# A two-layer cross-attention and feed-forward kernel: weight rows broadcast in two halves, second weights beside Gelu, last two tails transposed on TensorE, expert weights loaded a group earlier

## The chip, the cores and the metric

The kernel runs on one core of one Trainium2 chip, as one launch. The metric is device time in microseconds; the time of a kernel is the median of several executions. All arithmetic is in float32.

## The reference, cut to what matters

There are 16 sequences of 256 rows of width 256, `x`, and as many of context, `ctx`. Four stages follow one another, each added to the residual:

```
x = x + cross_attention_0(ctx, layernorm(x))   # 8 heads of 128; keys and values from ctx and x together (512 rows)
x = x + ffn_0(layernorm(x))                    # 256 -> 1024 -> 256, Gelu; see below
x = x + cross_attention_1(layernorm(x), ctx)   # one head of 256
x = x + experts(layernorm(x))                  # 8 gated experts of width 256, a weighted sum of those a row chooses
```

The first feed-forward has weights of its own for every sequence: to the shared `W1` and `W2` a small product of that sequence's own rows is added,

```
lt = y[:, 1:17, :];  even = lt[:, ::2];  odd = lt[:, 1::2]
m1 = (even[:, :4, :, None] * odd[:, :4, None, :]).reshape(B, 1024, 256)
m2 = (even[:, 4:, :, None] * odd[:, 4:, None, :]).reshape(B, 256, 1024)
h   = gelu(y @ W1.T + scale * y @ m1.T + b1)
out = h @ W2.T + scale * h @ m2.T + b2
```

so that sixteen rows of the normalised `y` have to be known everywhere before the feed-forward of that sequence can begin.

## The kernel before, in words

The order of the work on every engine is written out by the program; nothing is reordered at run time. The main loop goes over 128 heads, `n = 8 b + h`, sequence ("batch") after batch. For a head, `s0q` and `s0k` make queries and keys (TensorE tiles `pq`, `pk`), `s1` the scores (`sc`) and their maxima (`nm`, VectorE) and exponentials (`pr`, ScalarE), `s1_scale` divides the rows by their sums on GpSimd (L864), and `s2` transposes the result in blocks of 32 on VectorE into `tb` and sends it to DRAM (`hop`, L876); `s2_fetch` brings it back fully transposed (`pT`, four DMAs, L885), and `s3` multiplies it with the values (`po`, into `outT`). `tb` has one buffer: the next head's block transposes wait until the store of the one before has landed. `values` makes the values of half the heads at a time (`pv`), a tile at a time, as filler.

Between these steps the loop leaves gaps (`gap`), in which jobs run for the batches before: `chain(b)`, which carries batch b from the output projection (`px`) through both feed-forward matmuls (`ph`, `pf`), the second attention (`pv1`, `pq1`, `sc1`, `po1`) and the last layer norm, and `route(b)`, which picks experts and scatters rows with indirect DMAs from GpSimd (`slots_d`, L683). A job yields a number: the TensorE time, by the program's own count `Clock.pe`, after which its next step may be placed. `Clock.pe` is a planner's guess made when the program is built; on the chip each engine runs its own list in order and waits for semaphores. All plain DMAs are issued from one queue, SyncE's ("SP"), in order.

The chain of a batch transposes its four row blocks in the same way as the heads, by `to_blocks` (VectorE, then a store to DRAM) and `from_blocks` (four fetches): `yb` to `ybT`, `yc` to `ycT`, `pr1` to `pr1T`, `row` to `ydT`. The planner allows `SENT` = 6.5 us before the fetch and `LANDED` = 7.5 us after it.

For the first feed-forward the chain writes the sixteen rows of `y` to DRAM (`ev_d`) and reads them back into all 128 partitions, 8 KB each, by one DMA `ev<-ev_d` of 1 MB (L384). That DMA is issued right behind a head's four `pT` fetches, by the list `behind_fetch`. VectorE then builds the batch's first weights `W1e` (L412, two instructions for every two of the eight `ph` tiles) and GpSimd and VectorE its second ones, `W2e` (L419, L427), interleaved with the `ph` matmuls. Gelu (L459) is one ScalarE instruction over all of `hT`, and needs another activation table than the exponentials.

When the heads are done, the experts' part (`experts`) takes over TensorE: groups of up to four tiles of 128 rows, expert after expert, in two parts (the first ten batches, the last six). A group's rows are read from `slots_d` (L1091), transposed by the same hop over DRAM, and put through gate, up and down matmuls (`pg`, `pu`, `pd`); VectorE scales the result into a tile `o` (L1173), and GpSimd adds it to the output by an indirect DMA (L1174). An expert's weights `wx` are loaded two groups ahead of their use (L1074 to L1076). The rows of the second part may be loaded only when the last batch's `route` has scattered all of its slots. The chains of the last two batches run beside the first experts.

Of the kernel before, what the change touches and what calls it, by code (L numbers as in the profile page):

```python
# [12 lines left out]
F32 = mybir.dt.float32  # L13
# [6 lines left out]
P = 128  # L20
# [9 lines left out]
def xattn_ffn_kernel(  # L30
# [301 lines left out]
    def chain(b, A, behind):  # L332
# [8 lines left out]
        def mv_tile(tag):  # L341
            return small.tile([P, TC, 2], F32, tag=f"mv{tag}", bufs=2, name=f"mv_{tag}_{b}")

        def raw_tile(tag, name):
            return wk.tile([P, QP, DC, TC, QB], F32, tag=tag, name=name)

        mv = mv_tile("b")
# [25 lines left out]
        nc.vector.tensor_copy(yp, y[0:32, 0, :].rearrange("p (a c) -> p c a", c=NI))  # L373
        hop = to_blocks(wk, y, TC, "tbc", 1, f"yb_{b}_b")
        ev_d = dram.tile([2 * NI, D], F32, tag="ev_d", name=f"ev_d_{b}")
# [6 lines left out]

        def rows_everywhere():
            nc.sync.dma_start(  # L384
                ev.rearrange("p n d -> p (n d)"),
                ev_d.rearrange("n d -> (n d)").partition_broadcast(P),
            )
            landed.append(Clock.pe + 12.0)

        behind_fetch.append(rows_everywhere)  # L390
        plus_row(x_b, lasting["b2"])
        yield SENT
        yTb = raw_tile("yT", f"ybT_{b}")
        from_blocks(yTb, hop)
        yT = in_order(yTb)
        while not landed:
            yield 0.2
        yield max(landed[0] - Clock.pe, LANDED)
        while behind is not None and b - 1 not in A.fed_forward:
# [4 lines left out]
        nc.vector.tensor_scalar(  # L404
            od, yTb[:, 0, :, 0, 2 : 2 + 4 * NI : 2], lasting["scale"], None, ALU.mult
        )
# [25 lines left out]
        w1_rows(0)  # L432
        w2_block(0)
        w1_rows(1)
        yield 4.0 if b < B - 1 else 6.0
        hT = wk.tile([P, HC, S], F32, tag="hT", name=f"hT_{b}")
        for k in range(HC):
            ph = mm_tile(S, f"ph_{b}_{k}")
            for d in range(DC):
                mm(  # L440
                    ph, W1e[:, d].rearrange("p i a -> p (i a)")[:, ts(k, P)], yT[:, d],
                    start=(d == 0), stop=(d == DC - 1),
                )
            nc.vector.tensor_scalar(hT[:, k, :], ph, col("b1", k), None, ALU.add)
            if k % 2 == 1:
                i = k // 2
                if i + 2 < NI:
                    w1_rows(i + 2)
                if i + 1 < NI:
                    w2_block(i + 1)  # L450
                yield 1.0
                w2_add(i)
        A.fed.add(b)
# [8 lines left out]

        behind_exp.append(gelu)
        while not done:
            yield 0.2
# [24 lines left out]
        plus_row(x_b, lasting["bv1"])  # L490
        hop = to_blocks(wk, y, TC, "tbc", 1, f"yc_{b}_b")
        pr = wk.tile([P, TC, S], F32, tag="pr1", name=f"pr1_{b}")
# [5 lines left out]
        for m in range(TC):  # L498
# [4 lines left out]
            yield  # L503
        yield sent - Clock.pe
        yTc = raw_tile("raw_c", f"ycT_{b}")
        from_blocks(yTc, hop)
        landed = Clock.pe + LANDED + 1.5
        for c in range(TC):
# [3 lines left out]
            )  # L512
        yield landed - Clock.pe
        q1T = wk.tile([P, DC, S], F32, tag="q1T", name=f"q1T_{b}")
        for m in range(DC):
            pq = mm_tile(S, f"pq1_{b}_{m}")
            for d in range(DC):
                mm(
                    pq, M1[:, d, ts(m, P)], in_order(yTc)[:, d], start=(d == 0),
                    stop=(d == DC - 1),  # L520
                )
            evict(q1T[:, m, :], pq, u1[:, m : m + 1], QS1)
# [14 lines left out]
        yield 3.0  # L537
        hop = to_blocks(wk, pr, TC, "tbc", 1, f"pr1_{b}_b")
        yield SENT
        raw = raw_tile("raw_c", f"pr1T_{b}")  # L540
        from_blocks(raw, hop)
        yield LANDED
        pT = wk.tile([P, TC, S], F32, tag="pT1", bufs=1, name=f"pT1_{b}")
        for m in range(TC):
            evict(pT[:, m, :], in_order(raw)[:, m], None, None)
        yield 4.0
        mv = mv_tile("d")
# [14 lines left out]

        yield 2.8 if b < B - 1 else 10.0
        while b >= 2 and not A.tails[b - 2].done:
# [3 lines left out]
        nc.vector.tensor_copy(row[:, :, D + E], number[:, b * TC : (b + 1) * TC])  # L568
        hop = to_blocks(wk, row, TC, "tbc", 1, f"yd_{b}_b")
        yield SENT  # L570
        raw = raw_tile("raw_c", f"ydT_{b}")
        from_blocks(raw, hop)
        yield LANDED
        ydT = wk.tile([P, DC, S], F32, tag="q1T", name=f"ydT_{b}")
        for d in range(DC):
            evict(ydT[:, d, :], in_order(raw)[:, d], None, None)
        yield 4.0
        while b >= 1 and b - 1 not in A.weighed:
# [14 lines left out]
    def route(b, A, mine):  # L593
# [87 lines left out]
        for c in range(TC):  # L681
            for e in range(E):
                ins = nc.gpsimd.indirect_dma_start(  # L683
                    out=slots_d[part],
                    out_offset=bass.IndirectOffsetOnAxis(ap=at_slot[:, c, e : e + 1], axis=0),
                    in_=row[:, c, :], in_offset=None,
                )
                apart(ins, f"slots_{part}")
                if e % 2 == 1:
                    yield 2.6  # L690

# [11 lines left out]
    with ExitStack() as sh, ExitStack() as sa, ExitStack() as sf:  # L703
# [315 lines left out]
        def bulk(b, h):  # L1019
            if h == 0:  # L1020
                if b == 0:
                    filling["turns"] = all_turns()
                filling["in"] = inputs(b + 1) if b + 1 < B else None
            if h == 2:
                filling["v1"] = values(b, 1)
            if h == 6:
                filling["v0"] = values(b + 1, 0) if b + 1 < B else None
            if b == 0:
                load_late(h)
                for _ in range(2):  # L1030
                    advance(filling["turns"])
            if 2 <= h <= 5:
                advance(filling["v1"])
            if 1 <= h <= 5:
                advance(filling["in"])
            if h == 7 and b + 2 < B:
                load_in(b + 2)
            if h >= 6:
                advance(filling["v0"])
                yield  # L1040
                advance(filling["v0"])
            yield
# [35 lines left out]
        class G:  # L1078
# [83 lines left out]
            def down(self, t):  # L1162
# [4 lines left out]
                for i in range(IC):  # L1167
# [3 lines left out]
                    )  # L1171
                o = D_.wk.tile([P, D], F32, tag="o", bufs=8, name=f"o_{self.name}_{t}")
                nc.vector.tensor_scalar(o, pd, self.wt[:, t : t + 1], None, ALU.mult)  # L1173
# [9 lines left out]
        def experts(groups, ready=None):  # L1183
# [12 lines left out]
            for n, g in enumerate(groups):  # L1196
# [5 lines left out]
                for i in range(IC):  # L1202
                    g.gate(i)
                    yield
                    g.up(i)
                    yield
                    if n == 0:
                        groups[1].turn_rows(i)
                    if n + 2 < len(groups):
                        if i == 0:  # L1210
                            groups[n + 2].send_rows()
                        else:
                            groups[n + 2].fetch_rows()
                    if i == 0 and n + 3 < len(groups):
                        groups[n + 3].load()
                    if late is not None:
                        late.down(2 * i)
                        late.down(2 * i + 1)
                        yield
                if n + 2 < len(groups) and groups[n + 2].e not in D_.w:  # L1220
                    while len(D_.w) > 1 and D_.more is None:
                        yield 0.4
                    load_expert(groups[n + 2].e)
# [24 lines left out]
        for n in range(NS + 2):  # L1248
# [17 lines left out]
            while behind_exp:  # L1266
                behind_exp.pop()()
            stand = 2.0 if n >= NS - 1 else 0.0
            gap(stand=stand)
            if n < NS:  # L1270
                s1_scale(n)
            if 1 <= n <= NS:
                s2_fetch(n - 1)
            while behind_fetch:
                behind_fetch.pop()()
            if n + 1 < NS:
                s0q(n + 1)
            gap(stand=stand)
            if n + 1 < NS:
                s0k(n + 1)  # L1280
            gap(stand=stand)
            advance(more)
            gap(stand=stand)
            advance(more)
            gap(stand=stand)
            if n >= 2:
                s3(n - 2)
            gap(stand=stand)
            if n < NS:
# [4 lines left out]
        while line:  # L1294
            for late in (behind_exp, behind_fetch):
                while late:
                    late.pop()()
            if D_.more is None and B - 1 in A.projected:
# [52 lines left out]
```

## Time and profile before

| what | value |
|---|---|
| median of 3 runs | 1911.05 us (1908.29 to 1915.36) |
| the profiled execution | 1918.48 us, its span 1916.5 us |
| mean granted TensorE clock over the span | 0.978 |
| TensorE busy | 1837.2 us, 96% of the span |
| VectorE, ScalarE, GpSimd busy | 1215.9, 582.8, 864.8 us |
| bytes moved by DMA | 336.91 MB, mean 176 GB/s |

The profile tells for every instruction when it ran and how long its engine had been idle before, and what ended that idle time. A line of the timeline holds the start in us, the length in us, the engine, the source line, the operation, output and inputs by the program's names, and how many like it were merged; behind that, in brackets, the idle time before it and its releaser. SPq is SyncE's queue, which issues the DMAs. A helper records every matmul, so all have line L80 (transposes L84).

### The profile page before, as it was taken

The page shows a single profiled execution, that of the slowest core. Times are in us where ns is not written, and L with a number is a line of the kernel's source. Part 1 is how long each engine was busy: PE and PEld are TensorE (multiplying, and loading weights), DVE is VectorE, ACT ScalarE, POOL GpSimd, SP SyncE. Part 2 cuts the span into 40 slices and gives each one's busy share as a digit, 9 for nine tenths or more (in the row PEclk, how much of TensorE's full clock was granted, in tenths as well). Part 3 has the DMA queues.
Part 4 walks back from the last instruction along what each step waited for, and adds up shares of the span by engine and source line. Part 5 has one row for each costly group of instructions (what it writes and reads, how often), then busy time and mean ns, then how long its engine had stood idle before and what let it go on. Part 6 is the DMA issues. An engine that isn't in the chain of part 4 may idle for free. (4 is left out here: it accounts for less than half of the span.)

```text
span 1916.5 us, 22738 instructions
## 1 busy us (share of the span) xinstructions
PE 1837.2 (96%) x6568; PEld 1242.2 (65%) x6568; DVE 1215.9 (63%) x3350; ACT 582.8 (30%) x1297; POOL 864.8 (45%) x996
## 2 busy tenths in 40 slices
PE   8999999999999999899999999999998999998997
PEld 5666666666666666666666666666665766665665
DVE  5465676757676767576767676666665766664554
ACT  3333333333333333333333333333332211110110
POOL 2132325262626262526262626262615285776665
PEclk9999999999999999999999999999998999998998
DMA  6554446363646463636364636363636487998996
GB/s 223 177 176 139 157 132 201 132 202 127 213 132 205 136 208 132 198 126 211 127 211 138 206 132 203 133 206 134 210 107 208 136 226 197 250 255 201 209 208 109
DMA packets 274638, 336.91 MB, mean 176 GB/s; under 512 B 31773, under 2 KB 227273, under 8 KB 272457
## 3 DMA queue, kind: packets, MB, share of 16 engines
q1 hardware_dynamic: 243736, 283.82, 46.7%
q0 software_dynamic: 30720, 51.54, 11.5%
q8 instruction: 55, 0.90, 0.2%
q14 instruction: 79, 0.64, 0.1%
q10 hardware_dynamic: 48, 0.01, 0.0%
HBM read 167.87 MB, written 167.38 MB: 175 GB/s over the span
## 5 line engine op out<-in xcount | busy, mean ns | idle before, releaser
L864 POOL TENSOR_SCALAR pr<-pr,ri 128x512 f32<-128x512 f32 x256 | 178.0, 706 | 436.1 <-DVE ri L863 432.8
L856 ACT ACTIVATE pr<-sc,nm 128x512 f32<-128x512 f32 x256 | 173.7, 683 | 499.1 <-DVE nm L850 473.9
L683 POOL DMA_INDIRECT slots_d<-row,at_slot x256 | 254.7, 995 | 68.9 <-issue 67.9
L80 PE MATMUL po<-pT,v 128*128 128x256 f32 x1024 | 249.9, 388 | 4.0 <-DMA pT<-hop 4.0
L80 PEld LDWEIGHTS po<-pT,v 128*128 128x128 f32 x1024 | 201.3, 197 | 68.5 <-issue 33.2
L1174 POOL DMA_INDIRECT out_dram<-o,at x128 | 200.6, 1567 | 97.0 <-DVE o L1173 39.9
L80 PE MATMUL sc<-kT,qT 128*128 128x512 f32 x512 | 240.9, 593 | 0.0
L80 PE MATMUL pk<-kvT,Wk_sb 128*128 128x512 f32 x512 | 240.6, 592 | 0.0
L80 PE MATMUL pv<-Wv_sb,kvT 128*128 128x512 f32 x512 | 237.4, 592 | 0.0
L872 DVE STREAM_TRANSPOSE tb<-pr 128x512 f32<-128x512 f32 x256 | 165.7, 685 | 69.2 <-DMA hop<-tb 49.4
L80 PE MATMUL ph<-ybT,W1e 128*128 128x256 f32 x512 | 140.0, 418 | 38.0 <-DVE W1e L412 35.4
L850 DVE TENSOR_REDUCE nm<-sc 128x1 f32<-128x512 f32 x256 | 161.9, 666 | 15.8 <-PE sc L80 15.8
L80 PEld LDWEIGHTS pv<-Wv_sb,kvT 128*128 128x128 f32 x512 | 97.0, 190 | 102.2 <-issue 96.6
L80 PEld LDWEIGHTS ph<-ybT,W1e 128*128 128x128 f32 x512 | 103.7, 207 | 88.0 <-issue 65.5
L902 DVE TENSOR_SCALAR outT<-po,cvec 128x256 f32<-128x256 f32 x128 | 60.7, 474 | 149.2 <-PE po L80 118.3
L80 PE MATMUL pg<-yTd,wx 128*128 128x384 f32 (+3 forms) x328 | 127.8, 513 | 16.0 <-DVE o L1173 11.8
L80 PEld LDWEIGHTS pk<-kvT,Wk_sb 128*128 128x128 f32 x512 | 97.4, 190 | 68.0 <-issue 61.2
L80 PEld LDWEIGHTS sc<-kT,qT 128*128 128x128 f32 x512 | 97.0, 190 | 68.1 <-issue 61.2
L80 PE MATMUL pq<-kvT,Wq_sb 128*128 128x256 f32 x512 | 133.5, 383 | 0.0
L1149 ACT ACTIVATE sg<-pg 128x384 f32<-128x384 f32 (+3 forms) x82 | 41.3, 504 | 294.1 <-PE pg L80 239.6
L80 PE MATMUL pu<-yTd,wx 128*128 128x384 f32 (+3 forms) x328 | 126.2, 508 | 0.0
L80 PE MATMUL pd<-wx,hTd 128*128 128x256 f32 x512 | 124.3, 380 | 2.0 <-DVE hTd L1160 2.0
(191 smaller groups left out, 2659.1 us busy)
## 6 DMA issues: line engine op xcount, KB each, us to landing
hop<-tb SPq DMA_DIRECT2D x128, 512.0 KB
pT<-hop SPq DMA_DIRECT2D x512, 128.0 KB
ev<-ev_d SPq DMA_DIRECT2D x16, 1024.0 KB
rows<-slots_d SPq DMA_DIRECT2D x31, 397.5 KB
hop_rows_b<-rows_b SPq DMA_DIRECT2D x30, 384.0 KB
yTd<-hop_rows_b SPq DMA_DIRECT2D x120, 96.0 KB
rows<-slots_d SPq DMA_DIRECT2D x8, 530.0 KB
cin<-in_ctx_dram SPq DMA_DIRECT2D x16, 256.0 KB
```

The lines of the kernel that those rows point to most:

```text
L80: nc.tensor.matmul(out, lhsT, rhs, **kw)
L683: ins = nc.gpsimd.indirect_dma_start(out=slots_d[part], out_offset=bass.IndirectOffsetOnAxis(ap=at_slot[:, c, e : e + 1], axis=0), in_=row ...
L850: nc.vector.tensor_reduce(nm, sc, AX.X, ALU.max, negate=True)
L856: nc.scalar.activation(pr, sc, AF.Exp, bias=nm, accum_out=sm)
L864: nc.gpsimd.tensor_scalar(pr, pr, ri, 1.0, ALU.mult, ALU.mult)
L872: nc.vector.transpose(tb[:, :, c, :], heads[n][c][0].rearrange("p (m f) -> p m f", m=QP))
L902: nc.vector.tensor_scalar(o, po, col("bv", h), None, ALU.add)
L1149: nc.scalar.activation(self.sg, self.pg, AF.Tanh, scale=0.5)
L1174: ins = nc.gpsimd.indirect_dma_start(out=out_rows[0 : sum(NTOKS[: self.part + 1]), :], out_offset=bass.IndirectOffsetOnAxis(ap=self.at[:, ...
```

## The change

The broadcast `ev<-ev_d` becomes two DMAs of 512 KB, the rows for the first weights and those for the second, and `behind_fetch` gives out only one a head, so the second stands behind the next head's `pT` fetches. The building of `W2e` moves from between the `ph` tiles to behind the placing of Gelu. The `ph` tiles are planned 6.0 instead of 4.0 us behind the first `W1e` instructions. One tile of `values` moves from head 2 of each batch to head 5, which now places two. For the last two batches (`hopped` is false) the four hops over DRAM are replaced by `turned_tile`: four TensorE transposes into PSUM and one ScalarE copy each. `route` of the last two batches places its sixteen scatters at twice the distance. The experts' weights are loaded up to three groups ahead. `o` gets a ninth buffer, and the gaps in the last three steps of the loop take in at least 2.6 us of other work.

```diff
+        hopped = b < B - 2
+        def turned_tile(src, tag, name):
+            t = wk.tile([P, DC, S], F32, tag=tag, bufs=1, name=name)
+            nc.scalar.copy(t, transposed(src, f"{name}_p"))
+            return t
...
-        hop = to_blocks(wk, y, TC, "tbc", 1, f"yb_{b}_b")
+        if hopped:
+            hop = to_blocks(wk, y, TC, "tbc", 1, f"yb_{b}_b")
...
-        def rows_everywhere():
+        def rows_everywhere(half):
             nc.sync.dma_start(
-                ev.rearrange("p n d -> p (n d)"),
-                ev_d.rearrange("n d -> (n d)").partition_broadcast(P),
+                ev[:, ts(half, NI)].rearrange("p n d -> p (n d)"),
+                ev_d[ts(half, NI)].rearrange("n d -> (n d)").partition_broadcast(P),
             )
-            landed.append(Clock.pe + 12.0)
-        behind_fetch.append(rows_everywhere)
+            landed.append(Clock.pe + 8.0)
+        behind_fetch.extend([lambda: rows_everywhere(0), lambda: rows_everywhere(1)])
...
+            yield 2.2
+            yT = latents = turned_tile(y, "yT", f"ybT_{b}")
...
         w1_rows(0)
-        w2_block(0)
         w1_rows(1)
-        yield 4.0 if b < B - 1 else 6.0
+        yield 6.0
...
                     w1_rows(i + 2)
-                if i + 1 < NI:
-                    w2_block(i + 1)
                 yield 1.0
-                w2_add(i)
...
         behind_exp.append(gelu)
+        while len(landed) < 2:
+            yield 0.2
+        yield landed[1] - Clock.pe
+        for c in range(NI):
+            w2_block(c)
+            yield 1.7
+            w2_add(c)
...
+            yTc = turned_tile(y, "raw_c", f"ycT_{b}")
...
+            pT = turned_tile(pr, "pT1", f"pT1_{b}")
...
-        yield 2.8 if b < B - 1 else 10.0
+        yield 2.8 if b < B - 1 else 6.0
...
+            yield 1.4
+            ydT = turned_tile(row, "q1T", f"ydT_{b}")
...
                 if e % 2 == 1:
-                    yield 2.6
+                    yield 2.6 if b < B - 2 else 5.2
...
-            if h == 2:
+            if h == 3:
                 filling["v1"] = values(b, 1)
...
-            if h >= 6:
-                advance(filling["v0"])
+            if h >= 5:
+                late = filling["v1"] if h == 5 else filling["v0"]
+                if h >= 6:
+                    advance(late)
                 yield
-                advance(filling["v0"])
+                advance(late)
...
-                o = D_.wk.tile([P, D], F32, tag="o", bufs=8, name=f"o_{self.name}_{t}")
+                o = D_.wk.tile([P, D], F32, tag="o", bufs=9, name=f"o_{self.name}_{t}")
...
+                ahead = groups[min(n + 3, len(groups) - 1)].e
+                if ahead not in D_.w and (len(D_.w) < 2 or D_.more is not None):
+                    load_expert(ahead)
...
-            while behind_fetch:
-                behind_fetch.pop()()
+            if behind_fetch:
+                behind_fetch.pop(0)()
...
-            stand = 2.0 if n >= NS - 1 else 0.0
-            gap(stand=stand)
+            stand, least = (2.0, 2.6) if n >= NS - 1 else (0.0, 0.8)
+            gap(least, stand)
```

## The prediction, made before the changed kernel ran

> **What bounds the kernel now.** I read the page's busy shares first, then the waits of TensorE, then the timeline around the largest of them, then the tail. TensorE is busy 1837.2 of 1916.5 us, so only its idle time, and what follows from it, can be won. The list of its waits, by line and releaser:
>
> ```profile
> PE ph L80 <- DVE W1e L412: 35.4, 13, 5.0
> PE pg L80 <- DVE o L1173: 11.8, 2, 8.6
> ...
> PE pg L80 <- DMA wx<-in_L_ffn_Wg_dram: 4.1, 2, 2.7
> PE po L80 <- DMA pT<-hop: 4.0, 1, 4.0
> ```
>
> One wait recurs in nearly every batch: the first `ph` waits for its weights `W1e`. The timelines of three engines show why, in batch 5 (start, length):
>
> ```profile
> 593.66 0.36 SPq L384 DMA_DIRECT2D ev<-ev_d  x1
> 597.70 0.67 SPq L876 DMA_DIRECT2D hop<-tb  x1
> 604.98 1.76 SPq L885 DMA_DIRECT2D pT<-hop  x4
> 606.78 1.92 SPq L302 DMA_DIRECT2D pr1T<-hop_pr_b  x4
> 605.02 1.30 DVE L872 STREAM_TRANSPOSE tb<-pr 128x512 f32<-128x512 f32 x2 [4.56 <-DMA hop<-tb]
> 607.67 2.38 DVE L412 SCALAR_TENSOR_TENSOR W1e<-ev,od,W1T 128x256 f32<-128x256 f32 x4
> 604.07 1.88 PE L80 MATMUL pv<-Wv_sb,kvT 128*128 128x512 f32 x4
> 608.26 3.63 PE L80 MATMUL ph<-ybT,W1e 128*128 128x256 f32 x8 [2.31 <-DVE W1e L412]
> 613.60 1.89 PE L80 MATMUL po<-v,pT 128*128 128x256 f32 x8
> ```
>
> `ev` is issued at 593.66, the store `hop<-tb` behind it at 597.70. VectorE cannot write `tb` before that store has landed and waits 4.56 us for it, to 605.02. The maxima, `od` and `W1e` stand behind on VectorE, so `ph` starts 2.31 us late. Then comes a second loss: eight `ph` matmuls take 3.63 us where eight `po` take 1.89. The windows show the granted clock and the DMA share (columns: window, length, busy us and count of PE, PEld, DVE, ACT, POOL, then PEclk, DMA share, GB/s):
>
> ```profile
> 595.00:599.00 4.00, 4.00 (x13) 2.18 (x12) 1.70 (x5) 2.96 (x7) 3.08 (x4) 1.00 0.95 246
> 599.00:605.00 6.00, 6.00 (x20) 3.40 (x19) 0.48 (x1) 1.09 (x2) 4.89 (x7) 1.00 1.05 385
> 608.00:612.00 4.00, 3.74 (x9) 2.80 (x10) 2.75 (x8) 2.13 (x7) 2.98 (x5) 0.58 0.74 212
> 1463.00:1480.00 17.00, 10.88 (x29) 6.97 (x28) 7.73 (x18) 3.58 (x9) 8.15 (x10) 0.70 0.89 248
> 1747.00:1764.00 17.00, 8.43 (x22) 5.04 (x21) 5.63 (x15) 0.49 (x1) 14.13 (x10) 0.70 0.88 188
> ```
>
> The queues are full from 595 to 605, and from 608 to 612 the clock is 0.58. In the trace's clock records 11 of 13 batches (1 to 13) have such a spell at half speed behind the stall, nine of 3.41 and two of 6.83 us: 44.4 us, 22.2 lost. With 35.0 us idle in these batches the loop loses 57 us, 4.4 a batch.
>
> In the tail the same wait and the granted clock recur at 1463 (last batches), and the experts wait for rows:
>
> ```profile
> 1757.17 2.90 PE L80 MATMUL pg<-yTd,wx 128*128 128x384 f32 x4 [8.57 <-DVE o L1173]
> 1755.27 1.10 DVE L291 STREAM_TRANSPOSE rows_b<-rows 128x256 f32<-128x256 f32 x3 [11.97 <-DMA rows<-slots_d]
> ```
>
> The named releaser of the first line is VectorE, but VectorE itself sat 11.97 us until `rows` came, which may be read only after the last `slots_d` scatter: the DMA is the cause.
>
> **The halves and the moved tile.** Window 595 to 599 is the broadcast: some 4.3 us of a full queue. A half takes 2.1 us if time goes with bytes. Two things bring the `tb` store's landing forward: half the broadcast ahead of it (2.1), and the `pv` tile (1.72 us of pitch) that now stands in head 5, not head 2, so that heads 3 to 5 come that much earlier against the chain. Together 3.8 us, more than the 2.31 of the stall: `W1e` is then in time. What is next? On TensorE the order around here is now `pv`, `pv`, `po` of head 3, the second attention's `po1`, `sc`, and only then `ph`, while before `ph` came ahead of `po`. On SyncE half B stands behind the `pT` fetches of the next head and ahead of the four `pr1T` fetches. `po` would be due at 605.95, its `pT` landing at about 606.7: a wait of 0.75. `po1`, due at about 608.4, needs `pT1`, which ScalarE copies from `pr1T`:
>
> ```profile
> 611.53 0.71 ACT L787 COPY pT<-pr1T 128x256 f32<-128x256 f32 x2 [1.87 <-DMA pr1T<-hop_pr_b]
> ```
>
> That copy comes 3.8 us earlier by what is ahead, 2.1 later by half B: at 609.8, ending at 610.5, so `po1` waits about 2 us. The stall moves from `ph` to `po1`.
>
> I put the price on the whole loop by one point, the scores `sc` that follow this stretch. Over the 13 batches, the copy starts on average 18.3 us behind the issue of `ev`, and `sc` 22.5 us. In the changed order `sc` follows the copy by its first tile (0.4) and the two `po1` (1.73): 18.3 − 3.8 + 2.1 = 16.6 for the copy against the old issue, but that issue itself lies 1.7 later against the moved heads, so against the same point of the projection the copy is again at 18.3, and `sc` at 20.4. A wait that brings half speed like those in 11 of 13 batches adds 22.2/13 = 1.7, less the part that was already inside the 22.5 (0.25): 1.45, so 21.85. The gain is 0.67 a batch, 9 us over 13. Without half speed it is (22.5 − 20.4) × 13 = 28 us; if no wait were left at all it would be 57.
>
> Two rules of the Trainium skill speak to this. "DMA: Bandwidth & Descriptors", section "Anatomy of one DMA", gives a fixed 2.0 us beside bytes over 436 GB/s (fitted on the GpSimd path) and asks for DMAs of 1 MiB: by it a half is 3.2 us, an estimate, and the sum below would turn to about +6 us, no gain. The row against it is the window 599 to 605, where many smaller DMAs, one behind another, moved 385 GB/s: queued, fixed parts overlap, and I keep 2.1. "TensorE: Matmul & The Clock Gate", section "HAM oscillation", warns of PE idle gaps of over 3.4 us; by it waits of 2 us would not slow the clock and the loop would gain the 28. The row against it is the 2.31 us gap above, with 0.58 behind it; I keep the half speed.
>
> **`W2e` beside Gelu.** It takes GpSimd's scales and VectorE's four adds (group mean 0.78 us, 3.1 a batch) out of the `ph` tiles, and sets them behind. The cover is idle time: VectorE idles some 6.7 us from 630 to 643, GpSimd this long:
>
> ```profile
> 633.60 1.36 POOL L864 TENSOR_SCALAR pr<-pr,ri 128x512 f32<-128x512 f32 x2 [8.16 <-DVE ri L863]
> 645.34 1.36 POOL L864 TENSOR_SCALAR pr<-pr,ri 128x512 f32<-128x512 f32 x2 [10.37 <-DVE ri L863]
> ```
>
> I cost it at nothing; were the adds to stand ahead of a maximum that TensorE waits for, it would be 3.1 × 13 = 41 us. The 2 us more that the planner leaves before `ph` only reorder TensorE's list.
>
> **The tail.** From the rows of before, in profiled time:
> - 1463 to 1480: waits of 2.09 and 4.00 us and 17 × 0.30 = 5.1 of clock, 11.2 in all. The `pT` fetch was late behind the broadcast; half of it is there still. I take −3 (bounds 0 and −11).
> - Weights `wx` a group sooner: waits of 2.67 and 1.46 at 1546 and 1686, with 1.7 us of half speed behind the first: −5.9. Bounds 0 and −6.
> - Transposes on TensorE for two batches: four hops each, four tiles a hop, 32 tiles. The `cn_T` ones at 6.5 to 7.1 start 0.2 us apart at half speed, so 0.1 at full; one alone takes 0.27. I take 0.13, nearer the pitch: +4 (bounds 3 and 9). What they save is latency, which TensorE fills with experts. ScalarE's copies, 8 of 0.7 us, fall where it is busy a tenth or two: 0 to +1.
> - At 1584 `pg` waits 3.24, and 1.7 of clock follow. The new order has on GpSimd, ahead of a step that this wait turns on, 16 scatters at 1.28 pitch, six output adds at 1.85 and one scale of 1.0: 32.6 us, beside 29.1 of TensorE's work. So about +5 takes the place of −4.9: 0. Bounds −5 and +5.
> - The last scatter stands behind 57 rather than 60 output adds on GpSimd: 3 × 1.85 = 5.6 us sooner. Of the wait of 8.57 (13.7 with 17 × 0.30 of clock) 4.7 with its clock is left: −9. Bounds −14 and 0; the doubled distance of the scatters is in the count. The ninth `o` and the gaps of 2.6 I put at nothing; without a free `o` a wait of 0.84 (at 1739.87, VectorE) is the nearest row.
> Sum: −3 − 5.9 + 4 + 0 − 9 = −13.9, so −14.
>
> Loop and tail are −23: the profiled execution of 1918.48 would become 1895.5. It lies 7.4 us above the median of 1911.05, so the forecast is 1911 − 23 = 1888.
>
> **The rivals.**
> - *Stall moved to `po1`* (0.40): 1888, by its own unknowns 1875 to 1901.
> - *The waits left are too short for the clock, or vanish* (0.24): 1911 − 28 − 14 = 1869, at best 1911 − 57 − 14 = 1840. For it: two of 13 batches stalled without half speed. Against it: half B ahead of `pr1T`, and the 0.58 after only 2.31 us.
> - *It does not do what it says* (0.17): `W1e` comes no sooner because the `tb` store still waits behind fetches that keep the queue full to 605, and the tail gives only the weights' −6, with +4 for the transposes: 1909. For it: the share is 1.05 after the broadcast, too.
> - *Slower: a half takes as long as the whole* (0.19). Broadcast of 16 rows to 128 partitions, if each DMA has a price of its own: with δ us over 2.1 a half, half A delays the store and half B the `pr1T` fetches by δ each, and `po1` by 2δ in 13 batches. Break-even is 23/26 = 0.9, a half of 3.0 us; at 4.3 it is −23 + 26 × 2.1 = +32: 1943.
>
> **How the numbers follow.** About 0.5% (9.6 us) is what a measurement of this kernel can tell from no change: bounds 1901.5 and 1920.6. Faster: all but a part of the first and the second, 0.64; same: the third and a share of the others, 0.18; slower: most of the last, 0.18. The range from 1848 to 1925 leaves out the best end of the second case and the upper half of the last, about 2 in 10. The first case's own range is 1875 to 1901.
>
> **What would show it.** Right: the wait of `ph` for `W1e` nearly gone, `po1` waiting for ScalarE's `pT` about 2 us a batch with the clock near 0.6 behind it, `ev` halves of about 2 us, no wait for `wx`, a last wait for `rows` of about 5 us. Wrong: `po1` in time with full clock (second case), VectorE still waiting over 3 us for the `tb` store (third), a half with over 3 us of full queue (fourth), or new waits of TensorE for maxima behind the `W2e` adds.

## The result, and the profile after

The changed kernel took 1914.24 us (median of 12 runs, 1908.66 to 1922.22), the kernel before, run beside it, 1915.78 (12 runs, 1908.29 to 1925.62): a ratio of 0.9991, 95% interval 0.9968 to 1.0014. No change can be told. The forecast was 1888.

The profiled execution took 1912.54 us (before 1918.48), its span is 1910.8 us. TensorE's waits, first lines of the list (line and releaser: us in total, times, longest):

```profile
PE po L80 <- ACT pT L819: 24.5, 12, 3.1
PE po L80 <- DMA pT<-hop: 14.0, 9, 2.1
...
PE pf L80 <- DVE W2e L442: 6.0, 2, 4.2
...
PE pg L80 <- DMA wx<-in_L_ffn_Wg_dram: 3.7, 1, 3.7
PE pg L80 <- DVE yTd L823: 3.1, 1, 3.1
```

The wait of `ph` for `W1e` (35.4 us before) is gone. In its place `po` of head 3 waits for its `pT`, and the second attention's `po1` (also called `po` in the list, with ScalarE's `pT` as releaser) for the copy out of `pr1T`. In the tail two waits are new: the last batch's second feed-forward matmuls `pf` for `W2e`, and `pg` for `yTd`. Batch 5 again, from the timelines of TensorE, SyncE's queue, VectorE and ScalarE:

```profile
600.78 1.96 PE L80 MATMUL po<-pT,v 128*128 128x256 f32 x8 [0.65 <-DMA pT<-hop]
604.28 1.99 PE L80 MATMUL po<-v,pT 128*128 128x256 f32 x8 [1.53 <-issue]
595.52 1.74 SPq L917 DMA_DIRECT2D pT<-hop  x4
597.30 0.44 SPq L393 DMA_DIRECT2D ev<-ev_d  x1
597.79 1.94 SPq L302 DMA_DIRECT2D pr1T<-hop_pr_b  x4
595.54 1.30 DVE L904 STREAM_TRANSPOSE tb<-pr 128x512 f32<-128x512 f32 x2 [2.62 <-DMA hop<-tb]
603.82 0.71 ACT L819 COPY pT<-pr1T 128x256 f32<-128x256 f32 x2 [3.91 <-DMA pr1T<-hop_pr_b]
```

VectorE's wait for the store of `tb` is shorter (2.62, it was 4.56; over the whole profile these waits fell from 49.4 us to 30.5). Half B of `ev` stands between the two sets of fetches, ScalarE waits 3.91 us for `pr1T`, and `po1`, which needs that copy, starts 1.53 us late (the profile puts it down to issue).

I split each profiled execution at the last score matmul: the loop runs from the first score of batch 1 to the last score, the tail from there to TensorE's last matmul. Idle is the sum of TensorE's idle times over 0.1 us, half speed is half the length of the spells in the clock records (before the last 20 us).

| | loop us | idle | lost to half speed (spells) | tail us | idle | half speed |
|---|---|---|---|---|---|---|
| before | 1405.8 | 41.0 | 27.3 (12) | 410.3 | 18.6 | 8.5 |
| after | 1396.6 | 44.5 | 10.2 (6) | 409.7 | 14.8 | 8.5 |

The loop won 9.2 us. Half speed is the only column of the loop that fell, by 17.1; idle time rose by 3.5, and 4.4 us stand in neither column. The tail won 0.6. Outside these two stretches the changed kernel took 4.1 us longer, 1.3 ahead of the loop and 2.8 behind TensorE's last matmul; no term of the prediction and no run is about these.

The profiles differ by 5.9 us, the medians by 1.5. One kernel's executions differ in their clock: of the twelve of the changed kernel the fastest (1908.66) had a mean clock of 0.989, the slowest (1922.22) 0.979. This fits that waits near 1.5 to 2 us bring half speed in one execution and not in the next, but only one execution of each kernel was profiled.

### The profile page after: what moved, and what is told of

Same layout as the page of the kernel before. It is cut to its first block, busy times and chain, and to the rows that moved or that the text cites. A ratio compares the mean times of both kernels' runs of the same rounds, so it can differ in the third digit from the quotient of the medians.

```text
span 1910.8 us, 22717 instructions
## 1 busy us (share of the span) xinstructions
PE 1828.4 (96%) x6600; PEld 1236.7 (65%) x6600; DVE 1192.1 (62%) x3335; ACT 585.1 (31%) x1296; POOL 856.8 (45%) x996
## 4 chain that ended last, share of the span: by engine, by line
PE 74%; DMA 10%; DVE 5%; issue 4%; SPq 3%; POOL 2%; ACT 0%; ACTq 0%; DVEq 0%; POOLq 0%
PE po L80 10%; PE sc L80 9%; PE pv L80 8%; PE pk L80 8%; PE pf L80 6%; PE ph L80 6%; PE px L80 5%; PE pg L80 5%; PE pq L80 5%; PE pu L80 5%; PE pd L80 5%; DMA pr1T<-hop_pr_b 3%; DMA hop<-tb 3%; DVE tb L904 2%; SPq L302 2%
## 5 line engine op out<-in xcount | busy, mean ns | idle before, releaser
L80 PE MATMUL po<-pT,v 128*128 128x256 f32 x1024 | 242.8, 380 | 17.3 <-DMA pT<-hop 14.0
L80 PEld LDWEIGHTS po<-pT,v 128*128 128x128 f32 x1024 | 193.5, 190 | 82.6 <-issue 50.2
L904 DVE STREAM_TRANSPOSE tb<-pr 128x512 f32<-128x512 f32 x256 | 165.7, 685 | 35.5 <-DMA hop<-tb 30.5
L80 PE MATMUL pf<-W2e,hT 128*128 128x256 f32 x512 | 120.2, 383 | 6.0 <-DVE W2e L442 6.0
L80 PEld LDWEIGHTS pq<-kvT,Wq_sb 128*128 128x128 f32 x512 | 97.7, 191 | 43.0 <-issue 28.7
```

The lines of the kernel that those rows point to most:

```text
L80: nc.tensor.matmul(out, lhsT, rhs, **kw)
L904: nc.vector.transpose(tb[:, :, c, :], heads[n][c][0].rearrange("p (m f) -> p m f", m=QP))
```

## The experiments

All are timed against the kernel before on the same chip; ratios stand with 95% intervals. The kernel before took 1920.1 to 1926.4 us (medians) on these chips, so different experiments are compared by their ratios.

### The loop: where the second half stands, and the tile

**half_later.** One line. Only SyncE's list differs from that of the changed kernel, by the place of one DMA a batch.

```
- behind_fetch.extend([lambda: rows_everywhere(0), lambda: rows_everywhere(1)])
+ behind_fetch.extend([lambda: rows_everywhere(0), lambda: None, lambda: rows_everywhere(1)])
```

> Half B of the broadcast is issued one head later, behind the pT fetches of head 4 instead of head 3, so behind the pr1T fetches. Theory A (half B's own 2.1 us ahead of pr1T is what po1 waits for): po1's waits for ScalarE's pT, 24.5 us in 12 batches in the changed kernel, fall by about 2 us a batch, to under 6 us in all, with fewer spells at half speed; the time falls by 15 to 25 us against the changed kernel, to 1890 to 1900. Rival B (the queues are full through the whole stretch whatever the order, so somebody is late): the sum of TensorE's waits in the loop stays above 30 us, with the wait on another tile (pT of head 4, the tb store, or pf for W2e), and the time stays within 5 us of the changed kernel.

Measured: 1871.84 us, ratio 0.974 (0.9695 to 0.9786). Loop 1360.6 us, idle 17.7, half speed 3.4 (2 spells); tail as before, 412.5. Theory A's mechanism holds, and more was won than the 15 to 25 us that it said: 2.5% against the changed kernel, some 48 us by the ratios; in the profile's loop 26.8 us of idle time and 6.8 of half speed. The waits of the changed kernel were brought about by one DMA's place in the queue:

```profile
PE po L80 <- DMA pT<-hop: 10.0, 9, 2.2
PE pf L80 <- DVE W2e L442: 6.7, 2, 4.1
...
PE po L80 <- ACT pT L819: 1.5, 2, 1.3
```

**whole.** `ev` in one DMA again, in the place of half A.

> The changed kernel with the broadcast as one DMA of 1 MB again, all else as changed. Theory A (time goes with bytes, half A 2.1 us ahead of the tb store): the store lands about 2 us later in each batch, po's wait for pT<-hop grows from 14 us by 13 x 1.5 to 2 us, to about 35 us, po1's wait stays about as it is because as many bytes stand ahead of pr1T; the time is 5 to 20 us above the changed kernel. Rival C (every DMA of the broadcast has a price of its own, the halves cost more than the whole): the waits of po1 fall by over 1 us a batch, the time falls by 10 us or more.

Measured: 1913.83 us, 0.9971 (0.9943 to 0.9998). `po` waited 29.9 us for its `pT`, as theory A said. But the wait for ScalarE's copy did not stay: it came once (4.4 us), which is the sign that rival C named, without the 10 us. Idle was 41.4 and half speed 23.9 in the loop. So the waits move from one place to the other and the sum stays: the halves as the change places them (0.9991 against 0.9971) are worth nothing beyond noise.

**later_v1_back.** half_later with the `values` tile back in head 2.

> Half B one head later, and the values tile back in head 2, as before the change. Theory (the tile's 1.72 us bring heads 3 to 5 forward against the chain): po's wait for pT and the wait of ph for W1e grow by up to 1.7 us in each of 13 batches, with half speed behind some of them: the time is 10 to 30 us above that of half B later with the tile moved (1872). Rival (once half B is out of the way, there is slack for it): within 4 us of 1872.

Measured: 1913.57 us, 0.994 (0.9917 to 0.9963), 2.0% above half_later. The wait of `po` for `pT` grew to 33.2 us, 0.8 in the first of 12 batches and 1.9 to 3.7 in the others, with 12 spells. The 1.72 us tile stands just ahead of `po` of head 3 and covers its wait; without it the waits also pass the length that brings half speed: idle +20.6, half speed +18.8. (The planner also places other work of the loop anew around the moved tile, so the lists differ in more than this tile.)

**tile_only.** The same tile moved in the kernel before.

> The kernel before with one edit: the values tile moved from head 2 to head 5 of each batch. Theory (the tile's 1.72 us bring heads 3 to 5 forward against the chain, so the wait of ph for W1e shrinks by that): TensorE's waits in the loop fall from 41 to about 20 us and most get too short for half speed; the time falls by 20 to 40 us. Rival (the broadcast of 1 MB keeps the next transposes out whatever the tile does, and the wait turns up at po for its pT or at po1): the time is within 8 us of before.

Measured: 0.9973 (0.9953 to 0.9993). The rival holds. `ph` waited 34.2 us for `W1e`, as before: in this order the second tile stands behind the first `ph`, so nothing more covers that wait. Where the tile was seen to pay, in half_later against later_v1_back, TensorE's order is the other one, which the next runs are about.

### What W2e beside Gelu costs

**w2_only** is the kernel before with `W2e` moved behind Gelu, and `yield 6.0` ahead of `ph`; **plan_only** is that number alone, **w2_plan4** the move alone.

> The kernel before with one part of the change: W2e built behind the placing of Gelu for all batches, and the ph tiles planned 6.0 us behind the first W1e, the broadcast in one piece. Theory (the loop's idle time covers it, the last batch's does not): loop as before within 5 us, the last batch's pf waits 4 to 8 us for W2e with half speed behind: 3 to 10 us slower in all. Rival (the adds in the ph stretch held ph up, and taking them out shortens the loop): 5 to 15 us faster.

> The kernel before with one number changed: the first ph tiles planned 6.0 instead of 4.0 us behind the first W1e, in all batches. Nothing else is changed; TensorE's list then has po of head 3, sc of head 6 (and po1) ahead of ph, as in the changed kernel. Theory M (this order alone makes the loop longer, since po waits longer for its pT than ph waited for W1e): loop 25 to 40 us longer, TensorE's wait at po for pT<-hop 50 to 70 us in all, time 1.3 to 2.1% above before. Rival N (it is the moved W2e that does it, the order is worth nothing): within 5 us of before.

> The kernel before with W2e behind the placing of Gelu, but the first ph tiles planned 4.0 us behind W1e as before. Theory M: the loop is as before within 5 us, waits of ph for W1e of 30 to 40 us, only the last batch's pf waits for W2e, so the time is within 0 to +10 us of before. Rival N: 1.5 to 2% above before, as with both.

| | ratio | loop us | idle | half speed |
|---|---|---|---|---|
| w2_only | 1.0196 (1.0167 to 1.0224) | 1440.4 | 73.9 | 44.4 |
| plan_only | 1.0138 (1.007 to 1.0206) | 1440.6 | 72.3 | 44.4 |
| w2_plan4 | 0.9995 (0.9958 to 1.0033) | 1404.7 | 44.3 | 25.6 |

Theory M holds. w2_only came out 2.0% slower, outside both of its readings (3 to 10 us slower, 5 to 15 us faster), since neither had a price for the number 6.0. That one number makes the loop 35 us longer in the profile; the time of plan_only is up by 1.4%, some 27 us, and its profiled execution was the slowest of its four. With 4.0 the planner puts two `ph` tiles ahead of `po` of head 3, with 6.0 it puts `po` first, and that needs a transfer which is later still. plan_only's waits and one of its places:

```profile
PE po L80 <- DMA pT<-hop: 62.9, 12, 9.6
618.86 3.75 PE L80 MATMUL po<-pT,v 128*128 128x256 f32 x8 [5.88 <-DMA pT<-hop]
```

Before, `ph` waited 35.4 us there; now `po` waits 62.9. The move of `W2e` itself costs the loop nothing: w2_plan4's loop is as before, w2_only's as plan_only's. (w2_plan4's tail is 4.8 us longer than before.)

### What brings the half speed

**idle_work.** Ahead of the first `ph` of batches 1 to 13 the kernel before computes six matmuls on constants that nothing reads.

```
+ idle = mm_tile(S, f"idle_{b}")
+ for k in range(6):
+     nc.tensor.matmul(idle, M1[:, 0, 0:P], WvT[:, 0, :], start=(k == 0), stop=(k == 5))
```

> The kernel before, with six matmuls of 128x256 on constants, whose result nobody reads, put on TensorE right ahead of the first ph of batches 1 to 13, in the place of the wait; no other engine's list changes. They take 6 x 0.216 = 1.3 us each, 17 us of useless work in all. Theory H (half speed follows when TensorE was idle for over half of a 3.41 us stretch of a fixed grid): the 13 waits of 1.65 to 4.99 us become 0.4 to 3.7, only those of 3.3, 4.0 and 5.0, perhaps that of 3.24, are still long enough, so spells at half speed behind ph fall from 11 to 3 or 4, some 10 to 15 us are won, and the kernel with the useless work is 5 to 15 us faster. Rival I (the half speed comes from something else than TensorE's idle time: the load of the queues, or W1e itself): as many spells as before, time within 4 us of before. Rival J (the useless work is not hidden): 10 to 17 us slower.

Measured: 1909.49 us, 0.9925 (0.9896 to 0.9954): faster, with more work. My size of the work was wrong: each such matmul is two in the trace, so a batch got 2.75 us, 36 in all, not 17.

```profile
601.59 2.75 PE L440 MATMUL idle<-WvT,M 128*128 128x256 f32 x12
604.43 2.27 PE L80 MATMUL ph<-ybT,W1e 128*128 128x256 f32 x8
```

The loop's idle time fell from 41.0 to 14.1, its spells from 12 to 2, and the loop by 10.4 us. TensorE's idleness brings the half speed, as theory H says. In each trace the starts of the spells lie on a grid of 3.413 us, to within 0.01 us. How much idle time does it is read from windows of 3.41 us on this grid (columns as in the prediction). Two from before, then six of the changed kernel:

```profile
605.23:608.64 3.41, 1.10 (x4) 0.30 (x2) 3.38 (x7) 1.37 (x5) 1.35 (x3) 1.00 0.73 212
608.64:612.05 3.41, 3.41 (x9) 2.52 (x8) 2.16 (x7) 1.54 (x5) 2.39 (x4) 0.50 0.69 196
```

```profile
412.49:415.90 3.41, 1.97 (x8) 1.44 (x8) 0.55 (x2) 0.00 (x0) 2.38 (x3) 1.00 0.97 237
415.90:419.31 3.41, 1.89 (x9) 1.68 (x10) 0.68 (x2) 2.08 (x5) 0.00 (x0) 1.00 0.69 236
600.22:603.63 3.41, 1.96 (x8) 1.44 (x8) 0.56 (x2) 0.00 (x0) 2.94 (x4) 1.00 0.94 290
603.63:607.05 3.42, 2.77 (x11) 2.09 (x12) 1.43 (x5) 3.23 (x8) 0.26 (x1) 1.00 0.56 213
695.79:699.20 3.41, 1.50 (x8) 0.99 (x7) 0.55 (x2) 0.60 (x2) 1.57 (x2) 1.00 0.96 260
699.20:702.61 3.41, 3.41 (x9) 2.66 (x10) 1.14 (x4) 2.77 (x7) 0.00 (x0) 0.50 0.43 162
```

Busy 1.10 of 3.41 is followed by clock 0.50; busy 1.97 and 1.89, two windows running, is not (the window at 419.31 ran at 1.00), nor is busy 1.96; busy 1.50 (idle 1.91) is. The idle time of the two windows running comes from waits of 1.99 and 2.32 us, each of which lies across an edge of the grid; so it is not the length of a wait that counts, but what of it falls into one window. I counted this over the 16 traces of the case that have spells ahead of their last 20 us, for windows at full speed between 100 and 1830 us with over 0.5 us of idle time: of 187 with less than 1.6 us none was followed by half speed, of 42 between 1.6 and 2.0 eleven, of 154 with 2.0 or more all.

### The tail

**w2_last_early.** The changed kernel, with `W2e` of the last batch between its `ph` tiles as before.

> Only the last batch builds its second weights W2e between the ph tiles again, as before the change; the other batches as changed. Theory D (the last batch's W2e on GpSimd stands behind scatters and output adds, and pf waits for it): the two waits of pf for W2e, 6.0 us, and the half speed behind them, 3.4 us lost, go; the time falls by 5 to 9 us. Rival E (GpSimd's queue is the bound there whatever comes first): the waits reappear as waits for o, rows or ph within the same 40 us, and the time stays within 3 us.

Measured: 1902.54 us, 0.9903 (0.9869 to 0.9937). The tail took 399.3 us, 10.4 less; the waits of `pf` and their spell are gone. Theory D holds; the profiled executions differ by 9.5 us, the ratios by 0.9%, some 17 us, known to about 8. TensorE's list is the same in both kernels. In the changed kernel the waits, and what stands around a step of `W2e` on GpSimd, look like this:

```profile
1612.22 1.13 PE L80 MATMUL pf<-W2e,hT 128*128 128x256 f32 x4 [1.82 <-DVE W2e L442]
1617.54 6.18 PE L80 MATMUL pf<-W2e,hT 128*128 128x256 f32 x20 [4.19 <-DVE W2e L442]
1613.97 1.58 POOL L1208 DMA_INDIRECT out_dram<-o,at  x1 [0.30 <-issue]
1614.98 1.78 POOL L434 TENSOR_TENSOR W2e<-ev,od 128x256 f32<-128x256 f32 x2
```

**hopped_all** gives the changed kernel its hops over DRAM back; **turned_only** gives the kernel before the turned tails alone. Both keep the changed kernel's 6.0 for the 10.0 us that the planner left ahead of the last batch's `row`, and hopped_all keeps the doubled distance of the scatters.

> The four hops over DRAM are back for the last two batches too, all else as changed. If the turned tails are worth what they save in latency: the tail after the last scores becomes longer by 3 to 10 us, with waits of pg or of the experts' rows for the last scatter back near 5 to 8 us. If they cost only their 32 transposes and copies (about 4 us of TensorE) with the latency covered by experts' work: the time falls by 2 to 4 us or stays.

> The kernel before with one part of the change: the hops of the last two batches replaced by transposes on TensorE. Theory K (the turned tails are worth 15 to 22 us by themselves: the last scatter comes earlier and the wait of 8.57 us for rows with its half speed goes): the time falls by 8 to 20 us, in the tail alone. Rival L (they pay only beside the doubled distance of the scatters, else the scatters of two batches stand ahead of the output adds): within 4 us of before, with new waits for o or W2e on GpSimd's account.

Measured: hopped_all 1.0057 (1.0032 to 1.0083), tail 432.1 us, more than either reading said, with one wait of 14.5 us of `pg` for rows:

```profile
1774.18 2.26 PE L80 MATMUL pg<-yTd,wx 128*128 128x384 f32 x3 [14.48 <-DMA yTd<-hop_rows_b]
```

turned_only took 0.9914 (0.9883 to 0.9946), tail 404.9, with no such wait: theory K holds. Its median is 16 us down, its profile shows only 5.4 in the tail. The difference is one of which execution was profiled: that of turned_only (1912.62) lies 4 us above its median, that of the kernel before (1918.48) 6 us below the median of the runs beside turned_only (1924.74). The turned tails do pay; without them the rest of the change, with the planner's numbers that belong to them, would have lost.

**both** is half_later with the last batch's `W2e` early; **both_dist** has the scatters at single distance as well, **both_noahead** the experts' weights two groups ahead.

> Half B one head later and the last batch's W2e between its ph tiles. The two gains lie at different places (the loop; the last batch), so they should add: 1914 less 42 (half B later) less 10 (the last batch's W2e) = 1862, between 1857 and 1868. If the last batch's gain was in part the moving of work into a wait that half B later has removed, it would be 1868 to 1873.

> Half B one head later, the last batch's W2e between its ph tiles, and the scatters of the last two batches at the single distance again. Theory F (the doubled distance only delays the last scatter, for which the rows of the last experts wait): last scatter some 5 us earlier, time 0 to 5 us below that with the doubled distance. Theory G (at the single distance the scatters stand ahead of the output adds on GpSimd, and the experts wait for o): waits for o or hTd of 3 to 10 us come in the tail, time 3 to 10 us above.

> Half B one head later, the last batch's W2e between its ph tiles, and the experts' weights at most two groups ahead again, as before the change. If the earlier loads are worth what the prediction gave them (5.9 us): a wait of pg for wx of 1.5 to 2.7 us comes back at two places, some with half speed behind, and the time is 3 to 8 us above that with the earlier loads. Rival (the wait of 3.6 us for wx that the changed kernel has at the eighth group is there whatever is done later, as it comes from the opening of the third buffer): within 2 us.

Measured: both 0.9691 (0.9666 to 0.9716), 0.5% below half_later, which is about the noise of the two; against the changed kernel's 1914 it is 1857, the lower end of what was expected. Its tail is 8.5 us shorter than half_later's, so the second gain shows in the profile; that it adds in full is not shown. both_dist 0.9734 (0.9704 to 0.9763), theory G in sign, though its longest new wait was 5.8 us of a transpose for `yc`, not for `o`; both_noahead 0.9674 (0.9646 to 0.9702), no different from both. The earlier loads, which the prediction gave 5.9 us, bring nothing that can be measured.

**best4** is both_noahead with 4.0 instead of 6.0.

> Half B one head later, the last batch's W2e between its ph tiles, experts' weights at most two groups ahead (0.967 of before so far), and now the first ph tiles planned 4.0 us behind W1e again, so that ph and one values tile stand ahead of po of head 3. If the order is worth as much here as theory M says: po's waits for pT, 11.3 us, go; ph waits 0.2 to 0.8 us a batch for W1e; the time falls by 3 to 10 us. Rival (half A and the tile have made the order indifferent, or ph now waits over 1.7 us and brings half speed back): within 3 us, or 5 to 20 us slower.

Measured: 0.968 (0.9616 to 0.9745), not to be told from both_noahead. The wait of `po` for its `pT` is gone from its list, but `ph` and `po1` wait instead, 13.2 us of idle time against 14.2, and neither loop had a spell. With half B out of the way the order is indifferent. Both beat the kernel before by 3%.

## Why the prediction was wrong

The measured time lies inside the range (1848 to 1925), but a gain of 23 us was forecast and none came that can be told. In the profile 9.2 of 12 us came in the loop and 0.6 of 11 in the tail, and 4.1 were lost outside both.

- **The stall moves to `po1`: right.** Waits of 24.5 us over 12 batches for ScalarE's copy were what "about 2 us" a batch meant, with a smaller one at `po`. half_later shows that half B ahead of the `pr1T` fetches was the cause.
- **The loop's gain: near in sum, wrong in parts.** Forecast were 9, and 3 for the stretch at 1463, which lies in the loop and not in the tail; the starts of the scores show 6.1 ahead of 1459 and 3.1 behind. I kept half speed behind the stall and expected less idle time. Idle time rose by 3.5, half speed fell by 17.1, since the loss is spread over two waits a batch, most of them of 1 to 2.5 us. That the sum came near is in part luck. The second rival (waits too short for the clock) was half true.
- **"I cost it at nothing": the step that failed.** The cover for `W2e` was read in the loop and taken for the last batch too, where GpSimd has scatters and output adds: 10.4 us (w2_last_early). The price set against lost cover was a wait for maxima; it was `pf` that waited, 6.0 us, with a spell behind it.
- **"Only reorder TensorE's list": wrong as a price.** plan_only puts 35 us of loop on it. The forecast of the loop came near all the same, because it followed the score matmuls in the new order, in which `pv` covers `po`. That the tile and half A first had to pay back this order is a reading: no run has the changed kernel with 4.0.
- **Weights a group sooner, −5.9: mis-sized.** One wait of 3.7 us for `wx` stands in the place of two of 4.1, and both_noahead puts the whole at nothing. A wait of 3.1 us of `pg` for `yTd` was in no term; the timeline has two of batch 14's `W2e` adds among VectorE's work ahead of those copies, but no run took them away.
- **Transposes on TensorE, +4: taken as a cost alone.** The latency they save was said to be filled with experts. turned_only pays for the same 32 transposes and is 0.9% faster, and in hopped_all one wait for the rows behind the last scatter is 14.5 us.
- **Last scatter, −9: too small.** The wait of 8.57 us is gone entirely; VectorE waits 0.71 us for these rows:

```profile
1737.86 1.10 DVE L291 STREAM_TRANSPOSE rows_b<-rows 128x256 f32<-128x256 f32 x3 [0.71 <-DMA rows<-slots_d]
```

So of the −11 for the tail behind the last score, −0.6 came: 10.4 lost to the last batch's `W2e` and some 6 that the weights did not bring, against about 5 more at the last scatter.

- **Slower rival: not so.** A whole broadcast, 128 packets of 8 KB, took 3.9 us of the 16 DMA engines in the kernel before (packet times of the trace, summed and divided by 16; median of 16 batches). Half A and half B, read as the first 128 packets of 4 KB behind their issue, took 2.2 and 1.7 in the changed kernel. In this rival's own sum a half of 4.3 us is 2.2 above 2.1, not 2.1: 1945, not 1943. The weights' −5.9 is 5.8 by its rows. Neither of these two slips moves the forecast.
- **The ninth `o` and the gaps of 2.6 us**, put at nothing, were taken back by no run of the changed kernel.
- **The rule on the clock.** "TensorE: Matmul & The Clock Gate" ("HAM oscillation") speaks of idle gaps over some 3.4 us. Here the measurement decides: idle 1.91 us within one 3.41 us window was enough, and waits of 1.99 and 2.32 us that left 1.44 and 1.52 in neighbouring windows were not.

## What to carry to other kernels

In this kernel, where all plain DMAs stand in one full queue, splitting one was worth nothing until its second part stood behind what somebody waits for: with the same two halves the changed kernel was 0.1% below the kernel before with half B ahead of the `pr1T` fetches, and 2.6% with half B one head later. A wait has two prices, its length, and half speed once enough of it falls into one window, so price it per batch and not as a mean, and count filler ahead of it as cover. Read the cover of a moved step at each place where it will run, the last batch above all, and give a planner's number the price of the order that it makes.

## What the runs showed of the hardware

The clock's answer was sharper than expected: in these traces it depends on TensorE's idle time within windows of a fixed 3.41 us grid, with the limit between 1.6 and 2.0 us (none of 187 windows below, all of 154 above), and the next window (sometimes two or more) runs at 0.50. So 36 us of useless matmuls inside waits made a kernel 0.75% faster.
